# One-hots of the densest nodes and the clearing of their matrix: from VectorE to ScalarE

## The chip, the cores and the metric

The kernel runs on one core of one Trainium2 chip. The metric is the device time of one execution in microseconds (us); the figure for the kernel before is the median of 14 runs. A profile of one execution goes with it. Engines are named as in the profile: PE (TensorE, matrix products; PEld its weight loads), DVE (VectorE), ACT (ScalarE), POOL (GpSimd, which issues the indirect DMAs), SP (SyncE, which issues the plain DMAs). L971 is line 971 of the kernel before.

## What is computed

Four layers of a graph network over 12,500 nodes with 128 features and 200,000 edges; `dst` is sorted, and low-numbered nodes have many more incoming edges than high-numbered ones. Cut to what matters:

```python
edge_index = stack([src, dst])
x = layernorm(x + L0(x))     # h + out(sum over edges of filter(edge) * mlp(h)[src], at dst)
x = layernorm(x + L1(x))     # sum of x[dst] at src
x = layernorm(x + L2(x))     # sum of edge_weight * x[src] at dst, then two products, leaky relu
x = layernorm(x + L3(x))     # sum of alpha[rel] * (x @ w_rel[rel])[src] at dst, relu
```

The reference counts its layers from zero, and so do the kernel's `layers_0_and_1` and `layers_2_and_3` and this text. "Layer one" in the sense of whoever counts from one is layer zero here.

## The kernel before

**Groups and steps.** Edges go in 391 groups (`NG`) of 512 (four columns of 128, `J = 4`), from the last group to the first. `layers_0_and_1` is one long unrolled loop over steps `s`; in step `s` each stage works on another group, so that engines overlap. The order of instructions on each engine is the order in which the program issues them. An engine carries out its instructions in that order and waits at one whose inputs or buffers are not ready.

**Layer zero,** steps 0 to about 403. For the group that entered `k` steps ago: stage 2, PE computes `ph` (L783, one PSUM buffer); stage 3, ACT applies Silu (L766), and POOL gathers the source rows with four indirect DMAs (`gather`, L305) into one of seven `xg` buffers; stage 5, PE computes `pw` (L770, L773); stage 7, DVE writes the one-hots `oh` (L322) and multiplies `pw` by `xg` (L780), which frees that `xg` buffer; stage 8, PE sums by one-hots (L346); stage 11, DVE adds the result to `acc` (L371). So the gather for a group waits for the product L780 of the group seven before it. In the same loop 98 blocks of nodes are finished (`blk`, one every three steps or more), each with a Silu (L699), a square root (L639) and a scaling (L647) on ACT; Silu and square root need different tables, so each block brings two table loads. From step 21 on, 72 steps also start a DMA that fills `sums` with zeros out of a cleared part of `acc` (L403).

**Layer one,** from step 392 (`L1 = NG + 1`). For 308 groups ACT makes pairs of one-hots with `one_hots_on_act` (stage 2; L1013 to L1017: Abs, then Relu of one minus it, which is 1 where the difference is 0), PE multiplies them, ACT copies the result (`cnts`, L790, stage 5), PE multiplies again, ACT copies the messages (L833, stage 7) and POOL adds them to `sums` in DRAM with four indirect DMAs (`scatter_add`, L393, stage 8). The offsets of these, `to`, have nine buffers.

**The densest nodes.** The first 332 columns of 128 edges (`HC`) go to the nodes with the most edges. For them `DenseSteps` builds a matrix: for each column it makes two one-hots, `lo` (128 wide) for the source's place in its block and `hi` (490 wide) for the pair of source block and destination offset; PE multiplies them (L951), and DVE adds the product to a slice of `dense` (L962). `dense` is 128 partitions x 3136 f32. The columns come in 24 batches; after each, SP stores `dense` to DRAM (L967, 1568 KB) and DVE clears it (L971). This is done twice: with `kind` 0 in layer zero, where `hi` and `lo` are bf16 and the result is the plain counts for layer one; and with `kind` 1 in layer one, in f32 with the edges' weights, for layer two.

The constructor writes the order out by hand. A unit is one to four columns (or one column in two halves); one unit, or two that have four columns or fewer in all, starts every 1.68 steps for `kind` 0 and every 1.2 for `kind` 1. A unit is made in step `s`, multiplied in `s + 1`, added in `s + 2`. After the last unit of a batch, made in step `s`, the store is issued in `s + 3`, the clear in `s + 6` (`kind` 0) or `s + 5` (`kind` 1), and the next batch begins in `s + 5` or `s + 4`. `later` notes all this in two dictionaries: `taken` is run by `take` in the middle of a step, before ACT's one-hots of layer one and after its copy L790; `given` is run by `give` near the end, with `make` last. From the constants of the plan, `kind` 0 runs batches of

| batch | columns | made in steps |
|---|---|---|
| 0 | 72 | 8 to 36 |
| 1 | 28 | 41 to 51 |
| 2 | 22 | 56 to 64 |
| 3 | 18 | 69 to 75 |
| 4 | 16 | 80 to 91 |
| 5 to 23 | 176 | 96 to 365, at most 15 a batch |

For `lo` and `hi` there are four buffers each (tags `dense_lo` and `dense_hi`), one column a buffer. The lines of `make` that write them:

```python
lo = self.tile("dense_lo", P, dtype)
nc.vector.tensor_scalar(lo, c.row, ed.dense_lo[:, col:col + 1], None, op0=OP.is_equal)       # L930
hi = self.tile("dense_hi", J * P, dtype)[:, :NB * HW]
...
nc.vector.tensor_scalar(hi, self.key, ed.dense_key[:, col:col + 1], None, op0=OP.is_equal)   # L936
```

Of the kernel before, what the change touches and what calls it, by code (L numbers as in the profile page):

```python
# [8 lines left out]
F32 = mybir.dt.float32  # L9
BF16 = mybir.dt.bfloat16  # L10
I32 = mybir.dt.int32
AF = mybir.ActivationFunctionType
OP = mybir.AluOpType
# [4 lines left out]
P = 128  # L18
# [3 lines left out]
NB = 98  # L22
# [16 lines left out]
HS = 32  # L39
# [8 lines left out]
class Consts:  # L48
    def __init__(self, nc, pool):
        self.ident = pool.tile([P, P], F32, name="ident")  # L50
        make_identity(nc, self.ident)
        self.row = pool.tile([P, P], F32, name="row")
        nc.gpsimd.iota(self.row, pattern=[[1, P]], base=0, channel_multiplier=0,
                       allow_small_or_imprecise_dtypes=True)
        self.nodes = pool.tile([P, NB + 1], F32, name="nodes")
        nc.gpsimd.iota(self.nodes, pattern=[[P, NB + 1]], base=0, channel_multiplier=1,
                       allow_small_or_imprecise_dtypes=True)
        self.ones = pool.tile([P, P], F32, name="ones")
        nc.vector.memset(self.ones, 1.0)
        self.one_b = pool.tile([P, 1], BF16, name="one_b")  # L60
        nc.vector.memset(self.one_b, 1.0)
        self.eps = pool.tile([P, 1], F32, name="eps")
        nc.vector.memset(self.eps, EPS)

        self.before = pool.tile([P, P], BF16, name="before")
        nc.vector.tensor_scalar(self.before, self.row, self.nodes[:, 0:1], None, op0=OP.is_lt)
# [377 lines left out]
def kernel(ctx: ExitStack, tc: tile.TileContext, i, out):  # L444
    nc = tc.nc
    consts = ctx.enter_context(tc.tile_pool(name="consts", bufs=1))
    dram = ctx.enter_context(tc.tile_pool(name="dram", bufs=1, space=DRAM))
    c = Consts(nc, consts)
    ed = Edges(tc, c, i, consts)
# [28 lines left out]
    class Relations:  # L478
# [3 lines left out]
        def __init__(self, wk):  # L482
            self.comp = load_const(nc, wk, i["L3_gnn_compT"], [NBASIS, NREL], "comp", nc.scalar)
            self.flat = i["L3_gnn_weight"].rearrange("b d o -> b (d o)")
# [376 lines left out]
    class DenseSteps:  # L861
# [4 lines left out]
        def __init__(self, dn, ps, dense, fixed, first_weights, first_products):  # L866
            self.dn, self.ps, self.dense, self.fixed = dn, ps, dense, fixed
            self.key = dn.tile([P, NB * HW], F32, name="dense_row", tag="dense_row", bufs=1)
            nc.gpsimd.iota(self.key, pattern=[[1, NB * HW]], base=0, channel_multiplier=0,
                           allow_small_or_imprecise_dtypes=True)  # L870
            self.offs = Bases(nc.vector, ed.dense_off, "dense_off", HS - HW)
            self.degs = Bases(nc.vector, ed.dense_base, "dense_deg")
            self.rows = Bases(nc.sync, ed.dense_base, "dense_win")
            self.taken, self.given = {}, {}
            self.made, self.sums, self.ones = {}, {}, {}
            self.chunk, self.line, self.turned, self.at, self.out = {}, {}, {}, {}, {}

            for kind, t, apart, rate in ((0, 8.0, 4, 1.68), (1, first_weights, 3, 1.2)):
                for b, units in enumerate(DENSE):
                    k = 0  # L880
                    while k < len(units):
                        n = 2 if k + 1 < len(units) and units[k][1] * units[k + 1][1] and \
                            units[k][1] + units[k + 1][1] <= 4 else 1
                        s = int(t)
                        for u in units[k:k + n]:
                            self.later(self.given, s, self.make, kind, u)
                            self.later(self.given, s + 1, self.multiply, kind, u)
                            self.later(self.taken, s + 2, self.add, kind, u)
                        k += n
                        t += rate  # L890
                    self.later(self.given, s + 3, self.store, kind, b)
                    self.later(self.taken, s + apart + 2, self.clear)
                    t = s + 1 + apart
            for r in range(ROUNDS):
                start = first_products + r * (NB + 8)
                self.later(self.given, start - 3, self.load_rows, r)
                for k, h in enumerate(reversed(range(NB))):
                    if h % 2:
                        self.later(self.given, start + k, self.load, r, h - 1)
                    self.later(self.taken, start + k + 3, self.line_up, h)  # L900
                    self.later(self.given, start + k + 3, self.turn, h)
                    self.later(self.taken, start + k + 4, self.copy, h)
                    self.later(self.given, start + k + 5, self.product, h)
                    self.later(self.taken, start + k + 6, self.add_rows, h)
            self.end = max(max(self.taken), max(self.given))
# [17 lines left out]
        def make(self, kind, unit):  # L923
            c0, n = unit
            n = n or 1
            dtype = F32 if kind else BF16
            made = self.made[c0] = []
            for col in range(c0, c0 + n):
                lo = self.tile("dense_lo", P, dtype)
                nc.vector.tensor_scalar(lo, c.row, ed.dense_lo[:, col:col + 1], None, op0=OP.is_equal)  # L930
                hi = self.tile("dense_hi", J * P, dtype)[:, :NB * HW]
                if kind:
                    nc.vector.tensor_scalar(hi, self.key, ed.dense_key[:, col:col + 1], ed.dense_w[:, col:col + 1],
                                            op0=OP.is_equal, op1=OP.mult)
                else:
                    nc.vector.tensor_scalar(hi, self.key, ed.dense_key[:, col:col + 1], None, op0=OP.is_equal)  # L936
                made.append((lo, hi))
            if kind:
                ones = self.ones[c0] = self.dn.tile([P, J, HW], BF16, name="dense_one", tag="dense_one", bufs=4)
                for j in range(n):  # L940
                    nc.vector.tensor_scalar(ones[:, j, :], c.row[:, :HW], ed.dense_at[:, c0 + j:c0 + j + 1], None,
                                            op0=OP.is_equal)
# [24 lines left out]
            nc.sync.dma_start((weights if kind else counts)[b * P:(b + 1) * P, :],  # L967
                              self.dense.rearrange("p h n -> p (h n)"))

        def clear(self):  # L970
            nc.vector.memset(self.dense, 0.0)  # L971

        def load_rows(self, r):
            self.nodes = self.dn.tile([P, HK, D], F32, name="dense_x", tag="dense_x", bufs=1)
# [741 lines left out]
```

## Time and profile before

| what | value |
|---|---|
| median of 14 runs | 8075.14 us (8069.44 to 8083.61) |
| the profiled execution | 8082.02 us, its span 8080.2 us |
| busy: PE, DVE, ACT, POOL | 72%, 50%, 33%, 76% of the span |
| `lo` on DVE, L930, bf16 | 332 instructions, 293 ns each |
| `hi` on DVE, L936, bf16 | 332 instructions, 490 ns each |
| clear of `dense` on DVE, L971 | 48 instructions, 2672 ns each, 24 in each of the two layers |
| gathers of layers zero and two, L305 | 2796 instructions, 972 ns each |
| scatters of layer one, L393 | 1232 instructions, 1553 ns each |

Layer zero's gathers run from 78 to 2101 us, layer one's scatters from 2114 to 4421 us; layers two and three fill the rest. In a row of the timeline come start, duration (us), engine, line, operation, what it writes and reads, how many, and in brackets how long the engine was idle before it and what ended that. "issue" means that the profile shows nothing that the engine waited for. In a row of the waits come who waited, for whom, the sum in us, how often, and the longest.

### The profile page before, as it was taken

What the parts mean: (1) busy time and instruction counts of PE and PEld (TensorE: products, weight loads), DVE (VectorE), ACT (ScalarE), POOL (GpSimd) and SP (SyncE); (2) the same over time, 40 slices, a digit from 0 to 9 for tenths busy, and PEclk for the clock granted to TensorE, in tenths of its full rate; (3) what the DMA queues carried; (4) which work ended last, traced back from release to release, by engine and by line L of the source; (5) the groups of instructions that cost most, each with busy time, mean ns of one, the idle gap of its engine ahead of it and who ended that gap; (6) DMA issues with size and microseconds to landing.
All of it is one profiled execution on the core that took longest, in us unless ns stands there. A gap on an engine that the chain in (4) does not pass through costs nothing.

```text
span 8080.2 us, 89625 instructions
## 1 busy us (share of the span) xinstructions
PE 5827.1 (72%) x24309; PEld 3804.2 (47%) x24309; DVE 4070.6 (50%) x14132; ACT 2626.8 (33%) x5986; POOL 6117.8 (76%) x5603
## 2 busy tenths in 40 slices
PE   8889888888778766777643677777776666666665
PEld 5555555555445444554332345444443444444433
DVE  6776666554566555445431544545444443433333
ACT  2333333221578776777663311111110000000000
POOL 4777777777788888888887477777776777777777
PEclk8888878887888887777655888897875555555555
DMA  4543333333467677776665766664442222222222
GB/s 149 175 152 99 98 98 93 97 92 93 84 120 138 123 129 126 123 130 112 102 90 75 215 170 172 170 171 137 131 128 71 59 58 58 57 56 55 55 54 51
DMA packets 877254, 882.01 MB, mean 109 GB/s; under 512 B 428178, under 2 KB 683625, under 8 KB 870599
## 3 DMA queue, kind: packets, MB, share of 16 engines
q0 software_dynamic: 316960, 366.85, 25.1%
q1 hardware_dynamic: 545705, 496.90, 20.4%
q10 hardware_dynamic: 14078, 12.43, 0.5%
q8 instruction: 202, 3.31, 0.2%
q14 instruction: 309, 2.52, 0.1%
HBM read 555.71 MB, written 319.97 MB: 108 GB/s over the span
## 4 chain that ended last, share of the span: by engine, by line
POOL 27%; PE 20%; DMA 20%; issue 18%; DVE 10%; ACT 3%; DVEq 1%; SPq 0%; ACTq 0%; POOLq 0%
POOL xg L305 20%; POOL sums L393 7%; DMA xg<-table,at 6%; DMA sums<-xg,to 6%; DMA xg<-rel_table,at 6%; PE pa L346 5%; PE du L951 3%; PE pw L773 3%; PE pr L1161 2%; PE ph L783 2%; DVE dense L962 2%; DVE dense L971 1%; DVE acc L371 1%; DMA sums<-acc 1%; PE dense_sums L1212 1%
## 5 line engine op out<-in xcount | busy, mean ns | idle before, releaser
L305 POOL DMA_INDIRECT xg<-table,at x2796 | 2718.0, 972 | 953.1 <-issue 744.6
L346 PE MATMUL pa<-oh,xg 128*128 128x128 f32 x5592 | 1695.4, 420 | 1052.6 <-DMA xg<-rel_table,at 622.0
L393 POOL DMA_INDIRECT sums<-xg,to x1232 | 1913.5, 1553 | 414.1 <-issue 290.1
L346 PEld LDWEIGHTS pa<-oh,xg 128*128 128x128 f32 x5592 | 1192.2, 275 | 1636.2 <-issue 732.9
L305 POOL DMA_INDIRECT xg<-rel_table,at x1564 | 1483.4, 948 | 477.0 <-issue 370.9
L371 DVE TENSOR_TENSOR acc<-acc,pa 128x128 f32 x1090 | 305.9, 281 | 1453.6 <-PE pa L346 1403.4
L328 DVE TENSOR_SCALAR oh<-row,drel,wgt 128x128 f32<-128x128 f32 x2796 | 790.0, 357 | 36.3 <-PE pa L346 29.3
L951 PE MATMUL du<-dense_hi,dense_lo 128*128 128x490 f32 (+3 forms) x1239 | 701.8, 658 | 74.5 <-DVE dense L962 72.4
L647 ACT ACTIVATE x<-x,off,rs 128x128 f32<-128x128 f32 x294 | 144.9, 493 | 1373.0 <-DVE off L646 1363.2
L830 PE MATMUL fixed<-oh,one_b 128*1 128x128 bf16 x1216 | 145.0, 256 | 596.3 <-DVE m L1021 592.1
L783 PE MATMUL ph<-dt,fw 50*128 50x512 f32 x782 | 503.6, 728 | 79.1 <-ACT h L766 71.3
L773 PE MATMUL pw<-fw,h 128*128 128x128 f32 x3128 | 555.9, 332 | 0.0
L773 PEld LDWEIGHTS pw<-fw,h 128*128 128x128 f32 x3128 | 469.2, 230 | 118.9 <-issue 118.6
L346 PE MATMUL pa<-oh,m 128*128 128x128 f32 x3128 | 505.4, 315 | 11.0 <-DVE acc L371 10.9
L346 PEld LDWEIGHTS pa<-oh,m 128*128 128x128 f32 x3128 | 473.9, 232 | 12.4 <-DVE acc L371 11.8
L639 ACT ACTIVATE rs<-mv,eps 128x1 f32<-128x1 f32 x294 | 86.8, 295 | 1205.5 <-DVE mv L634 1187.5
L962 DVE TENSOR_TENSOR dense<-dense,du 128x490 f32 x646 | 427.8, 662 | 90.1 <-PE du L954 70.1
L1013 ACT ACTIVATE oh<-row,drel 128x128 bf16<-128x128 f32 x1216 | 388.6, 394 | 222.5 <-PE fixed L830 220.6
L1026 DVE TENSOR_TENSOR to<-n_ahead,at 128x4 int32<-128x4 f32 x308 | 50.6, 164 | 809.3 <-DMA sums<-xg,to 803.2
L780 DVE TENSOR_TENSOR m<-pw,xg 128x512 f32<-128x512 f32 x391 | 267.7, 685 | 365.2 <-DMA xg<-table,at 345.7
L766 ACT ACTIVATE h<-ph,fb 128x512 f32<-128x512 f32 x391 | 266.6, 682 | 533.5 <-PE ph L783 531.6
L1161 PE MATMUL pr<-wrel,x 128*128 128x512 f32 x784 | 429.0, 675 | 2.3 <-ACT x L1153 2.3
(205 smaller groups left out, 8449.4 us busy)
## 6 DMA issues: line engine op xcount, KB each, us to landing
rel_table<-tb SPq DMA_DIRECT2D x196, 512.0 KB
dt<-in_src_r SPq DMA_DIRECT2D x308, 256.0 KB
xg<-table,at POOLq DMA_INDIRECT x2796
dt<-in_dfT SPq DMA_DIRECT2D x391, 100.0 KB
dense_counts<-dense SPq DMA_DIRECT2D x24, 1568.0 KB
dense_in<-dense_counts SPq DMA_DIRECT2D x98, 384.0 KB
dense_weights<-dense SPq DMA_DIRECT2D x24, 1568.0 KB
dense_w_in<-dense_weights SPq DMA_DIRECT2D x96, 384.0 KB
```

Source lines behind the costliest of these rows:

```text
L305: nc.gpsimd.indirect_dma_start(out=x[:, j, :], out_offset=None, in_=table, in_offset=bass.IndirectOffsetOnAxis(ap=idx[:, j:j + 1], axis=0))
L328: nc.vector.tensor_scalar(oh[:, j, :], c.row, at[:, j:j + 1], weight[:, j:j + 1], op0=OP.is_equal, op1=OP.mult)
L346: self.nc.tensor.matmul(pa, x[:, j, :], oh[:, j, :], start=j == 0, stop=j == J - 1)
L371: nc.vector.tensor_add(to, to, pa)
L393: nc.gpsimd.indirect_dma_start(out=accs[(first + j) % len(accs)], out_offset=bass.IndirectOffsetOnAxis(ap=to[:, j:j + 1], axis=0), in_=msg ...
L773: nc.tensor.matmul(pw[:, j, :], h[:, j * P:(j + 1) * P], w.fw2, start=False, stop=j == J - 1)
L780: nc.vector.tensor_mul(ms[g], pws.pop(g), xgs.pop(g))
L783: nc.tensor.matmul(phs[g], w.fw1, dts.pop(g), start=True, stop=True)
L951: nc.tensor.matmul(pk[:, :NB * HW], lo[part], hi[part], start=j == 0, stop=j == len(made) - 1)
L962: nc.vector.tensor_tensor(to, to, pk[:, :NB * HW].rearrange("p (h n) -> p h n", n=HW), op=OP.add)
L1013: nc.scalar.activation(pair[:, 0, j, :], c.row, AF.Abs, bias=at[:, j:j + 1], scale=-1.0)
L1161: nc.tensor.matmul(pr, t["x3"], wrel[:, k:k + 4, :], start=True, stop=True)
```

## The change

In `make`, for `kind` 0 alone, DVE's two comparisons a column become four activations on ACT: for `lo` and for `hi`, the absolute difference, and then in place Relu of one minus that. For `kind` 1 the two comparisons stay on DVE. In both kinds the clear of `dense` becomes two copies on ACT of a constant zero column, one for each half of the matrix (1568 elements a partition each); the first half is cleared one step earlier than the whole was, the second half in the step in which the whole was.

```diff
+        self.zero = pool.tile([P, 1], F32, name="zero_c")
+        nc.vector.memset(self.zero, 0.0)
...
-                    self.later(self.taken, s + apart + 2, self.clear)
+                    self.later(self.taken, s + apart + 1, self.clear, 0)
+                    self.later(self.taken, s + apart + 2, self.clear, 1)
...
                 lo = self.tile("dense_lo", P, dtype)
-                nc.vector.tensor_scalar(lo, c.row, ed.dense_lo[:, col:col + 1], None, op0=OP.is_equal)
                 hi = self.tile("dense_hi", J * P, dtype)[:, :NB * HW]
                 if kind:
+                    nc.vector.tensor_scalar(lo, c.row, ed.dense_lo[:, col:col + 1], None, op0=OP.is_equal)
                     nc.vector.tensor_scalar(hi, self.key, ed.dense_key[:, col:col + 1], ed.dense_w[:, col:col + 1],
                                             op0=OP.is_equal, op1=OP.mult)
                 else:
-                    nc.vector.tensor_scalar(hi, self.key, ed.dense_key[:, col:col + 1], None, op0=OP.is_equal)
+                    for to, of, at in ((lo, c.row, ed.dense_lo), (hi, self.key, ed.dense_key)):
+                        nc.scalar.activation(to, of, AF.Abs, bias=at[:, col:col + 1], scale=-1.0)
+                        nc.scalar.activation(to, to, AF.Relu, bias=c.ones[:, 0:1], scale=-1.0)
...
-        def clear(self):
-            nc.vector.memset(self.dense, 0.0)
+        def clear(self, k):
+            half = self.dense.rearrange("p h n -> p (h n)")[:, k * NB * HS // 2:(k + 1) * NB * HS // 2]
+            nc.scalar.copy(half, c.zero.to_broadcast([P, NB * HS // 2]))
```

## The prediction

> **What bounds the kernel now.** I read the page first, then the waits of GpSimd, then its instructions one by one. The page's busy shares and the first line of its chain:
>
> ```profile
> PE 5827.1 (72%) x24309; PEld 3804.2 (47%) x24309; DVE 4070.6 (50%) x14132; ACT 2626.8 (33%) x5986; POOL 6117.8 (76%) x5603
> POOL 27%; PE 20%; DMA 20%; issue 18%; DVE 10%; ACT 3%; DVEq 1%; SPq 0%; ACTq 0%; POOLq 0%
> ```
>
> POOL is 76% busy and the chain gives it 27% plus 18% of "issue". The waits of POOL and of DVE in layer zero (95 to 2070 us) say what "issue" is:
>
> ```profile
> POOL xg L305 <- issue: 404.7, 1328, 0.3
> DVE m L780 <- DMA xg<-table,at: 326.4, 165, 7.7
> ```
>
> POOL sits 0.3 us before each gather and never longer: a fixed price, not a wait. A gather is 0.944 + 0.305 = 1.25 us, four make a group, so POOL cannot do a step under 5.0 us; 391 steps are 1955 of the 1975 us. POOL bounds layer zero, and the product L780 waits for what it fetches. ScalarE is far from the bound, ACT 45 us busy in 119 to 260 us. So work that leaves DVE pays only if it reaches POOL. One thing does:
>
> ```profile
> L305 POOL DMA_INDIRECT xg<-table,at x1527: 940/944/4134, 94.3 to 2069.5; - x191
> L393 POOL DMA_INDIRECT sums<-xg,to x1209: 1541/1542/1862, 2128.9 to 4398.9; - x173
> ```
>
> and two rows of the timeline (start, duration, engine, line):
>
> ```profile
> 1190.77 4.10 POOL L305 DMA_INDIRECT xg<-table,at  x1 [0.30 <-issue]
> ...
> 1191.31 2.67 DVE L971 MEMSET dense<- 128x3136 f32 x1 [0.60 <-issue]
> ```
>
> The first fence has min/median/max of the gathers (layer zero) and of the scatters (layer one). A gather has a median of 0.944 us and a maximum of 4.13. In the timeline 22 gathers are over 2.2 us; each overlaps one of the 24 memsets of `dense`, and 22 of 22 end 0.9 us after it: 1190.77 + 4.10 = 1194.87 against 1191.31 + 2.67 = 1193.98. Together they are 58.6 us over the median. The memsets at 266.8 and 419.8 stretched nothing, nor did any of the 24 in layer one, where no scatter is over 1.86 us.
>
> **Part 1, the clears.** DVE loses 48 memsets of 2.67 us. In layer zero that gives POOL 58.6 us back if the copy on ScalarE does not hold it. Nearest row: gathers that ran beside ScalarE's Abs and Relu at 2078 to 2100 us took 0.94 us. So I book -59, with 0 as the other end.
> Here the Trainium skill speaks against the row. "SBUF — State Buffer", section "Who interferes with whom", has VectorE and GpSimd share one port pair as an exclusive lock, but says that on this chip an instruction with one SBUF input or none, outside the two-port modes, does not contend, and names a memset as contending on trn3 alone. By that rule there is no relief, and the sum below would be 8195. The trace shows 22 of 24, so I follow it. The same section has ScalarE wait for nobody.
>
> **Part 2, the one-hots.** Of 332 columns DVE loses 0.29 + 0.49 us each (L930, L936), 260 us, from an engine that waits 326 us for gathers: worth nothing. ScalarE gets four activations a column. Their price, from rows of the same Abs and Relu at the start of layer one:
>
> ```profile
> 2077.86 0.69 ACT L766 ACTIVATE h<-ph,fb 128x512 f32<-128x512 f32 x1 [2.56 <-PE ph L783]
> 2078.45 1.26 ACT L1013 ACTIVATE dense_hi<-row,drel 128x128 bf16<-128x128 f32 x4
> 2079.62 1.26 ACT L1015 ACTIVATE dense_hi<-dt,src_f 128x128 bf16<-128x128 int32 x4
> 2080.91 1.15 ACT L1017 ACTIVATE dense_hi<-dense_hi,ones 128x1024 bf16<-128x1024 bf16 x1
> 2081.97 0.28 ACT L806 ACTIVATE past<-at,nodes 128x4 f32<-128x4 int32 x1
> ```
>
> Abs follows Silu without a table load. Four narrow ones take 1.26 us, one alone 0.39 (group row L1013), so the next independent one starts after (1.26 - 0.39) / 3 = 0.29. The Relu that reads them starts 0.03 after their end. Per element, (1.148 - 0.388) / 896 = 0.85 ns, so 490 wide is 0.388 + 362 x 0.00085 = 0.69, and 0.60 to the next independent one. A column: 0.42 + 0.29 + 0.72 + 0.60 = 2.03 us. Bounds: 1.78 if nothing waits for an Abs to end, 2.16 if nothing overlaps.
> "ScalarE: Activation LUTs", section "What ACT_TABLE_LOAD costs", states 280 ns + 0.833 ns per element with a pointer bias and 93 ns of overlap back to back. That makes an estimate of 1.78 us a column, a loss of 63 us below in place of 100 and a time of 8099; the row at 2080.91 shows that Relu waits, so 2.03 stands.
>
> Where does it lie? The columns are bunched: 72 in steps 8 to 36, then 28 (41 to 51), 22 (56 to 64), 18 (69 to 75), 16 (80 to 91), and under 1.3 a step later. The stretch of the first batch, by windows (PE, PEld, DVE, ACT, POOL; clock, DMA):
>
> ```profile
> 101.00:236.00 135.00, 127.93 (x663) 82.06 (x662) 102.34 (x355) 37.30 (x54) 102.39 (x108) 0.93 0.46 135
> ```
>
> ScalarE there has 37 us. Batch 0 becomes 72 x 2.03 = 146, + 37, + 13 of waits = 196 us, where POOL needs 29 x 5.0 = 145: 51 over. The waits: only four columns' buffers exist, so of 18 units the six made one step after the last wait for PE to do ph (1.12) and its first product (0.42), some 1.7 us each with the handover, and 3 us elsewhere. Likewise, with the same windows' ACT time and 3 us for the clear before: batch 1 57 + 21 + 3 + 5 = 86 against 55, batch 2 45 + 16 + 3 + 4 = 68 against 45, batch 3 37 + 11 + 3 + 3 = 54 against 35, batch 4 32 + 25 + 3 + 2 = 62 against 60. Over: 51 + 31 + 23 + 19 + 2 = 126 us.
>
> What is queued behind: the Silu of the next group stands behind these activations on ScalarE, the next ph and pw behind it on PE, the product L780 behind those on DVE, and only that frees a buffer for POOL. POOL's cover is seven buffers: the product of group 8 (in order of processing) ends at 139.2 and the gather that reuses its buffer starts at 153.6, so the lead is 14 us at the start (28 at most later, and 5.6 for group 68, at 451). Between batches are four steps in which PE can run at 4.0 us (Silu 119.51 to 167.88 in 12 steps) against POOL's 5.0, so some 12 us are made up in three gaps. Loss for POOL: 126 - 14 - 12 = 100 us. At the lower price without the waits, the overruns are 20 + 19 + 13 + 11 and the loss 37; at 2.16 with nothing made up between batches it is 126 + 156 x 0.13 - 14 = 132. After step 92 ScalarE needs some 80% of a step, the lead grows again, and nothing more is lost; what was lost is not got back, since POOL has no idle time left in layer zero.
>
> **Part 3, the clears in layer one.** POOL is the bound again (scatter 1.54 + 0.31, four in 7.4 us). ScalarE is 312 of 400 us busy at 2300 to 2700 and now stops for the store of `dense`: its first half comes a step earlier than the memset did, right after the copy L790. In three batches the memset itself waited, so landing is known: 2303.27 to 2310.82, 2515.41 to 2523.52, 2594.87 to 2603.09, about 8 us after issue. L790 ends 0.5 to 6.6 us after the issue, so ScalarE waits 7, 2, 2, 8 and 7 us in the first five batches, 26, plus 15 of copying (1568 elements at 0.85 ns + 0.2 = 1.5 us a half). Queued behind it are the one-hots, and the message copy L833 that POOL waits for. At that time messages are 3 to 9 us ahead of POOL; later 25 to 35, enough for any such stop. Of 41 us I book half, 20; bounds 0 and 41. No scatter was held by a memset, so no relief here. Layers two and three are untouched. The added constant is one small memset before the bound starts: nothing.
>
> **Sum.** -59 + 100 + 20 = +61 us. The profiled execution took 8082.0 us (span 8080.2), 6.9 over the median of 14 runs, 8075.1; span 8141, runs 8136 us.
>
> **Rivals.**
> Faster: the overrun is absorbed. If ScalarE's batches fit (seven buffers, DVE out of PE's way, Relu not waiting), only the relief is left: 8075 - 59 = 8016. For it: the 22 stretched gathers are certain, and DVE held PE up (L951 waits 72.4 us for L962). Against: 72 columns at the lower price are 128 + 37 = 165 us in 145. It decides where a column costs under (145 + 14 - 37) / 72 = 1.69 us; the sign turns already where loss and stops together stay under 59.
> Even: a loss near 50 and no stop in layer one cancel the relief, 8065 to 8085.
> Slower still: the copy on ScalarE, or the one-hots left around it, hold gathers as the memset did: no relief, 8136 + 59 = 8195. Against: gathers at 2078 to 2100.
> That the edit does not do what it says would show as L930 and L936 still on DVE in layer zero; the diff leaves them no path there.
>
> **How the numbers follow.** My forecast (relief, and ScalarE over its steps) 0.69, 8136, own range 8050 to 8190. Faster rival 0.14; even 0.08; slower still 0.09. Its low end is 37 - 59 + 0 = -22, 8053; its high end 132 - 59 + 41 = +114, 8189. The range goes to 8045 and 8205 to take in the slower rival. What a measurement here can tell from no change is about 0.2%, 16 us (the runs spread over 14). Faster 0.18 (its rival and the low edge of mine), same 0.10, slower 0.72.
>
> **What the profile of the changed kernel would show.** Right: no gather over 1.4 us beside a clear; POOL waits of microseconds before L305, released by L780, between 150 and 600 us, some 100 us in all and none after; ACT at nine tenths in the slices to 500 us; Silu L766 there 7 us apart; layer zero ending some 40 us later; in layer one ScalarE waiting for `dense_weights` and new gaps of POOL before 2700. Wrong: POOL without such gaps (then the first rival), or gathers still stretched to 3 or 4 us at the clears (then the last), or ScalarE loading tables between Silu and Abs, which no row here shows.

## The result, and the profile after

The changed kernel takes 8159.12 us (median of 6 runs, 8150.81 to 8168.44) against 8077.2 us for the kernel before beside it: the ratio is 1.0101, 95% interval 1.0091 to 1.0111. It is slower by 82 us; the forecast was 61, and the range held it. The profiled executions differ by a little less: spans of 8153.8 and 8080.2 us, 73.6 us apart. Lines have moved: L305 is now L307, L780 is L782, L766 is L768, L783 is L785, L393 is L395, L833 is L835; the activations are L941 (Abs) and L942 (Relu), the clear is L979.

The page of the changed kernel, its busy shares, two rows of its slices (203.8 us each) and the first line of its chain:

```profile
PE 5878.6 (72%) x24309; PEld 3831.5 (47%) x24309; DVE 3751.2 (46%) x13421; ACT 3417.3 (42%) x7410; POOL 6049.1 (74%) x5603
...
ACT  5878775544467887777664311111110000000000
POOL 4457777777788888888888377777776777777777
...
POOL 25%; PE 20%; DMA 19%; issue 17%; ACT 11%; DVE 7%; DVEq 1%; SPq 0%; ACTq 0%; POOLq 0%
```

DVE lost 319 us of comparisons and memsets, ACT gained 790 us and stands at seven and eight tenths from the second to the sixth slice, and POOL, which bounds the kernel, is at four and five tenths in the second and third slice, where it had seven. The chain goes through ACT for 11% where it had 3%.

The gathers of layer zero and the scatters of layer one (min/median/max in ns, first and last start in us):

```profile
L307 POOL DMA_INDIRECT xg<-table,at x1549: 938/944/1042, 94.7 to 2175.9; - x194
```
```profile
L395 POOL DMA_INDIRECT sums<-xg,to x1232: 1541/1542/1981, 2190.3 to 4502.5; - x176
```

No gather in this view is over 1.04 us any more: the relief came, and a little more of it than forecast. The waits of POOL from 95 to 2200 us say what it was spent on:

```profile
POOL xg L307 <- issue: 413.9, 1358, 0.3
POOL xg L307 <- DVE m L782: 138.4, 43, 8.1
POOL xg L307 <- DVE acc L373: 25.9, 21, 8.2
```

The fixed 0.3 us before each gather is there as before; new are 138.4 us of waits for the product L782 and some that are put down to `acc`. Gap by gap, what exceeds 0.31 us before a gather sums to 0.0 us before and 144.7 us after, in 34 gaps. Counted along POOL, layer zero is 66.5 us better (stretched gathers 58.6 to 0, small excesses over 0.944 us 11.3 to 3.4) and 144.7 worse. Compared group by group, the changed kernel is behind by 9 us after 24 groups of four gathers, 48 after 40, 109 after 64, 133 after 88, and then gains back to 76 at the last, as the stretches that it no longer has fall due. In layer one the distance stays 76 us from the first scatter to the last (before, these started at 2113.7 and 4426.6 us).

The first batch in windows (columns as shown before), and ACT's own waits over batches 0 to 4:

```profile
99.80:313.90 214.10, 161.12 (x662) 97.99 (x662) 64.99 (x228) 179.92 (x343) 123.77 (x131) 0.76 0.32 94
```

```profile
ACT h L768 <- PE ph L785: 40.8, 23, 3.9
ACT hb L701 <- DVE x L708: 35.4, 12, 8.9
ACT dense_lo L941 <- PE du L957: 25.4, 12, 3.5
ACT x L649 <- DVE off L648: 12.1, 5, 3.3
```

ACT is busy 179.9 of 214.1 us in the stretch that had been 145 us, and in the 580 us of the five batches it waits 114 us, 66 of them for PE. How this reaches POOL is seen in the longest waits of PE and of DVE, from 100 to 660 us:

```profile
PE ph L785 <- ACT h L768: 127.9, 36, 8.7
DVE acc L373 <- PE pa L348: 245.4, 41, 10.3
```

Before, from 95 to 590 us, the two were 34.7 and 59.2 us. PE waits for ACT's Silu; the sums `pa` stand behind `ph` in PE's order; DVE stands at the add of `pa` to `acc`, and behind that add stands L782, which frees the gather's buffer. L782 does not wait for its own input: before each of the 34 gaps its `pw` had been done for 8 to 20 us.

How ACT and PE hold each other up is seen in the timeline where one unit of four columns ends (first ACT's rows alone, then some rows of each engine):

```profile
206.06 0.39 ACT L941 ACTIVATE dense_lo<-row,dense_lo 128x128 bf16<-128x128 f32 x1
206.48 0.40 ACT L942 ACTIVATE dense_lo<-dense_lo,ones 128x128 bf16<-128x128 bf16 x1
206.78 0.69 ACT L941 ACTIVATE dense_hi<-dense_row,dense_key 128x490 bf16<-128x490 f32 x1
207.51 0.70 ACT L942 ACTIVATE dense_hi<-dense_hi,ones 128x490 bf16<-128x490 bf16 x1
208.12 0.39 ACT L941 ACTIVATE dense_lo<-row,dense_lo 128x128 bf16<-128x128 f32 x1
...
213.19 0.69 ACT L768 ACTIVATE h<-ph,fb 128x512 f32<-128x512 f32 x1
213.92 0.94 POOL L307 DMA_INDIRECT xg<-table,at  x1 [1.01 <-DVE m L782]
213.93 2.07 PE L785 MATMUL ph<-dt,fw 50*128 50x512 f32 x2 [5.38 <-ACT h L768]
215.93 1.41 PE L957 MATMUL du<-dense_hi,dense_lo 128*128 128x490 bf16 x3
...
216.56 0.40 ACT L941 ACTIVATE dense_lo<-row,dense_lo 128x128 bf16<-128x128 f32 x1 [2.68 <-PE du L957]
```

A column takes 2.06 us, from 206.06 to 208.12. The whole unit, with the two table loads behind it, delays the Silu of the next group to 213.19; PE had waited 5.38 us for it, and then the one PSUM buffer of `ph` lets PE do one product and no more. ACT in its turn waits 2.68 us for the products L957 that free a `dense_lo` buffer. Neither can work ahead of the other.

In the runs e5 to e8 and e12 the kernel before took 9176 us in place of 8074 to 8078, as DVE waited for something outside the profile ("remote", 689 us before L371 in e6) and POOL had some 600 us of gaps in layer zero; from these I read only single gathers and scatters, and layer one, where POOL's gaps are 23 to 30 us as in the other runs.

### The profile page after: what moved, and what is told of

Its sections match the earlier page's. It is cut to its first block, busy times and chain, and to the rows that moved or that the text cites. A ratio compares the mean times of both kernels' runs of the same rounds, so it can differ in the third digit from the quotient of the medians.

```text
span 8153.8 us, 90401 instructions
## 1 busy us (share of the span) xinstructions
PE 5878.6 (72%) x24309; PEld 3831.5 (47%) x24309; DVE 3751.2 (46%) x13421; ACT 3417.3 (42%) x7410; POOL 6049.1 (74%) x5603
## 4 chain that ended last, share of the span: by engine, by line
POOL 25%; PE 20%; DMA 19%; issue 17%; ACT 11%; DVE 7%; DVEq 1%; SPq 0%; ACTq 0%; POOLq 0%
POOL xg L307 18%; POOL sums L395 7%; DMA sums<-xg,to 6%; DMA xg<-table,at 5%; DMA xg<-rel_table,at 5%; PE pa L348 5%; PE du L957 3%; PE ph L785 3%; PE pw L775 3%; PE pr L1169 2%; ACT dense_hi L942 2%; ACT dense_hi L941 1%; DVE dense L968 1%; ACT dense_lo L942 1%; ACT h L768 1%
## 5 line engine op out<-in xcount | busy, mean ns | idle before, releaser
L307 POOL DMA_INDIRECT xg<-table,at x2796 | 2650.4, 948 | 1097.7 <-issue 750.7
L395 POOL DMA_INDIRECT sums<-xg,to x1232 | 1912.3, 1552 | 415.0 <-issue 286.5
L307 POOL DMA_INDIRECT xg<-rel_table,at x1564 | 1483.6, 949 | 477.1 <-issue 375.5
L957 PE MATMUL du<-dense_hi,dense_lo 128*128 128x490 f32 (+3 forms) x1239 | 710.6, 669 | 28.1 <-DVE dense L968 28.0
L785 PE MATMUL ph<-dt,fw 50*128 50x512 f32 x782 | 516.2, 744 | 200.3 <-ACT h L768 192.6
L768 ACT ACTIVATE h<-ph,fb 128x512 f32<-128x512 f32 x391 | 266.6, 682 | 391.5 <-PE ph L785 390.2
L782 DVE TENSOR_TENSOR m<-pw,xg 128x512 f32<-128x512 f32 x391 | 267.3, 684 | 317.4 <-DMA xg<-table,at 288.5
```

Of the source, the lines that this page charges most:

```text
L307: nc.gpsimd.indirect_dma_start(out=x[:, j, :], out_offset=None, in_=table, in_offset=bass.IndirectOffsetOnAxis(ap=idx[:, j:j + 1], axis=0))
L395: nc.gpsimd.indirect_dma_start(out=accs[(first + j) % len(accs)], out_offset=bass.IndirectOffsetOnAxis(ap=to[:, j:j + 1], axis=0), in_=msg ...
L768: nc.scalar.activation(hs[g], phs.pop(g), AF.Silu, bias=w.fb1)
L785: nc.tensor.matmul(phs[g], w.fw1, dts.pop(g), start=True, stop=True)
L957: nc.tensor.matmul(pk[:, :NB * HW], lo[part], hi[part], start=j == 0, stop=j == len(made) - 1)
```

## The experiments

No run leaves out any of the work. Each ratio is to the kernel before as it ran beside: 8074.15 us for e1 to e4, 8077.52 for e9 to e11, 9176 for the others.

The theory after the result: ACT's units of four columns hold up layer zero's first 92 steps, and the clears on ACT give the relief. Rivals: the latency that four activations in place of two comparisons add to each column; a cost of each moved column wherever it lies; and, for the relief, that something other than the memset held the gathers.

### Each part alone (e1, e2)

e1, the clears alone; e2, the one-hots alone, with the memset back on DVE:

```diff
# e1, against the change
-                    for to, of, at in ((lo, c.row, ed.dense_lo), (hi, self.key, ed.dense_key)):
-                        nc.scalar.activation(...)   # Abs, Relu
+                    nc.vector.tensor_scalar(lo, c.row, ed.dense_lo[:, col:col + 1], None, op0=OP.is_equal)
+                    nc.vector.tensor_scalar(hi, self.key, ed.dense_key[:, col:col + 1], None, op0=OP.is_equal)
# e2, against the change
-            nc.scalar.copy(half, c.zero.to_broadcast([P, NB * HS // 2]))   # two halves
+            nc.vector.memset(self.dense, 0.0)                              # one clear
```

> The clears on ScalarE as in the change, the one-hots of the counts back on VectorE. My theory: the memset on VectorE is what held the gathers, so no gather is over 1.4 us, POOL never waits for L780, and the time is that of before less 59 to 67 us: 8010 to 8018. Rival 1, the relief in the changed kernel came from the one-hots that left VectorE, not from the clears: gathers are stretched as before or half as much, 8045 to 8077. Rival 2, ScalarE's stop for the store of the matrix costs layer one what the prediction booked: 20 us more, 8030 to 8038.

> The one-hots on ScalarE as in the change, the clears back on VectorE in one memset, at their old step. My theory: the loss of 145 us by ScalarE's overrun in steps 8 to 92 stays whole, and the gathers beside the memsets after step 92 are stretched as before (some 50 us; the earlier ones fall where POOL is held anyway): 8200 to 8225. Rival, ScalarE's clears and their wait are a good part of the overrun: the gaps of POOL before L305 fall to 120 us or less and the time to 8170 to 8195.

e1 took 8026.11 us, ratio 0.9937 (0.992 to 0.9954): 48 us faster than the kernel before, and 8 us short of what I expected. In its trace no gather of layer zero takes over 1.23 us, POOL has no gap there, and the layer ends 57 us earlier. e2 took 8171.44 us, ratio 1.0118 (1.0102 to 1.0135). Its gaps sum to 138 us of the change's 145, so the loss is the one-hots'. But I had expected 50 us of stretch with the memsets back, and there were 21.8, in 9 gathers of 24 memsets. The maximum shows that the stretch is there:

```profile
L307 POOL DMA_INDIRECT xg<-table,at x1548: 938/944/4055, 95.3 to 2191.2; - x194
```

In the timeline of e2 one memset that stretched nothing, and one that did (rows of DVE and POOL):

```profile
540.64 2.67 DVE L976 MEMSET dense<- 128x3136 f32 x1 [0.60 <-issue]
541.12 0.94 POOL L307 DMA_INDIRECT xg<-table,at  x1 [0.30 <-issue]
542.37 0.94 POOL L307 DMA_INDIRECT xg<-table,at  x1 [0.30 <-issue]
543.23 0.23 DVE L708 SCALAR_TENSOR_TENSOR x<-x,fixed 128x128 f32<-128x128 f32 x1
...
766.73 2.67 DVE L976 MEMSET dense<- 128x3136 f32 x1 [0.60 <-issue]
767.25 3.04 POOL L307 DMA_INDIRECT xg<-table,at  x1 [0.30 <-issue]
769.32 0.75 DVE L324 TENSOR_SCALAR oh<-row,drel 128x128 f32<-128x128 f32 x4
```

The memsets are the same, 0.60 us after the add to `acc`. What differs is the next instruction of DVE: 0 of 15 memsets followed by a reciprocal or a scalar_tensor_tensor held a gather, 9 of 9 followed by a tensor_scalar did. Before, all 24 memsets of layer zero had a tensor_scalar behind them (L930, once L322) and all 24 of layer one a tensor_tensor. That made a new question, taken up below.

### Where the loss comes from (e3, e4, e7, e11)

e3: `lo` on ACT, `hi` on DVE. e4: the change, with a unit of batches 0 to 3 every 2.5 steps. e7 and e11, the same kernel: the columns below 156 on DVE.

```diff
# e3
+                    nc.scalar.activation(lo, ...)   # Abs, Relu
+                    nc.vector.tensor_scalar(hi, self.key, ed.dense_key[:, col:col + 1], None, op0=OP.is_equal)
# e4
-                        t += rate
+                        t += rate if kind or b > 3 else 2.5
# e7, e11
-                if kind:
+                if kind or col < 156:
```

> As the change, but only the narrow one-hot (128 wide) is made on ScalarE; the wide one (490) stays on VectorE. A column costs ScalarE some 0.72 us in place of 2.06, so the first batch needs 72 x 0.72 = 52 + 37 = 89 us in 145. My theory, the loss is work over the step: nothing is lost and the time is that of the clears alone, 8010 to 8020. Rival, the loss is latency, since what PE waits for now stands behind Silu in ScalarE's order: a third or more of the 145 us stays, 8060 or more.

> As the change, but the first four batches of the counts start a unit (or pair) every 2.5 steps in place of 1.68, which moves the later batches back by some 29 steps. The first batch then has 45 steps, 225 us, for 146 of one-hots, some 58 of the rest and some 20 of waits. My theory, the loss is ScalarE's work over the steps given to it: it falls from 145 to under 25 us, 8010 to 8040. Rival, the loss comes with each column, by the order of waits between ScalarE and PE, however far apart the columns lie: the gaps of POOL stay over 70 us, 8085 or more.

> The change, with the columns below 156 (batches 0 to 4, the bunched ones of steps 8 to 91) made on VectorE as before; the 176 later columns and all clears stay on ScalarE. Theory (the loss comes only from steps in which four columns hold ScalarE for 8.2 us at over 1.3 columns a step): no gap of POOL over 5 us in all in layer zero, the relief stays whole, 8020 to 8032 us. Rival (each column moved costs something wherever it lies): 176 of 332 columns keep half of the loss, 60 to 80 us, 8085 to 8110 us.

> The change with the columns below 156 made on VectorE, once more, for its time on another chip: no gap of POOL over 5 us in all in layer zero, ratio 0.993 to 0.9955. Rival (each column moved costs something wherever it lies, 176 of 332): ratio 1.001 to 1.005.

e3 took 8027.94 us (ratio 0.9938, 0.9922 to 0.9955), with no gap of POOL: half of the work on ACT costs nothing, though what PE needs for a column still stands behind the Silu in ACT's order, so a latency from that order alone falls. e7, beside 9176 us, gave 0.999 (0.9968 to 1.0012) and decides nothing. e11 took 8018.69 us (0.9928, 0.9911 to 0.9944). POOL's waits in its layer zero, 95 to 2030 us, hold nothing over 0.3 us:

```profile
POOL xg L307 <- issue: 404.1, 1326, 0.3
POOL xg L307 <- DMA xg<-table,at: 15.5, 51, 0.3
POOL xg L307 <- DVE oh L324: 15.5, 51, 0.3
POOL xg L307 <- DVE acc L373: 5.5, 18, 0.3
```

So 176 of 332 columns, with all four activations each, are free on ACT, and the other 156, the bunched ones, carry the whole loss. The free ones come one or two to a step: such steps take 5.5 and 6.6 us in e11, and the lead on POOL, over 12 us there, takes that up.

e4 took 8101.8 us (ratio 1.0034, 1.0021 to 1.0046), against the 8010 to 8040 that I expected; it is what the rival on record for it had, 8085 or more with gaps over 70 us. Spread to 2.5 steps, the four columns and the rest of ACT's work are 4 x 2.06 + 2.5 x 1.3 = 11.5 us in 12.5, and yet POOL lost 87 us in gaps:

```profile
POOL xg L307 <- issue: 393.8, 1292, 0.3
POOL xg L307 <- DVE m L782: 82.2, 34, 8.0
POOL xg L307 <- DVE acc L373: 22.9, 24, 6.9
```

The table tells why. It counts the steps from 8 to 109 (Silu to Silu) by the columns made in them:

| kernel | steps with 4 columns | mean us | steps with none | mean us | ACT busy in these |
|---|---|---|---|---|---|
| before | (DVE) | | 102 | 4.99 | 1.69 |
| change | 34 | 10.8 | 50 | 3.45 | 1.64 |
| e4 | 34 | 9.9 | 64 | 3.76 | 1.8 |
| e3 (`lo` alone) | 34 | 6.7 | 50 | 3.63 | 1.64 |

A unit falls into one step. That step takes some ten microseconds, and a step without columns is not over when ACT's 1.64 us are done, but after 3.45 in the mean (1.9 to 9.8); PE is busy for 2.9 of these. How much of them is PE's own work, held up before, and how much the passing of the group to and fro was not measured apart. PE's work also grew: in the windows of the first batch 662 products took 161.1 us of it, and 663 took 127.9 before, at a granted clock of 0.76 against 0.93. So the time of a stretch is not ACT's work in it summed, but that of its steps one by one. For the change, 34 x 10.8 + 50 x 3.45 + 123 for the 18 steps with one to three columns = 663 us, where POOL needs 102 x 5.0 = 510; less the lead of 14, a loss of 139, measured 144.7. For e4, 34 x 9.9 + 64 x 3.76 + 30 for four more = 607, less 510 and 14: 83, measured 87.3. For e3 the same sum is 34 x 6.7 + 50 x 3.63 + 95 = 504, under 510: no loss. These are sums of measured steps: they show that POOL's gaps are what the long steps cost over its pace less what the short ones give back, and forecast nothing. A unit spread evenly over its steps, the direct test, was not tried. Not tried either was the DMA that fills `sums` with zeros out of `acc`: DVE's add to `acc` waited 57.6 us for it from 100 to 660 us, against 40.6 in all of layer zero before; in e3 it waited 40.9 us and POOL lost nothing.

### What held the gathers (e5, e10, e6, e9, e12, e8)

Each is the kernel before, with one instruction behind the memset, or another one in its place:

```diff
             nc.vector.memset(self.dense, 0.0)
+            nc.vector.reciprocal(self.plug, c.ones[:, 0:1])                        # e5, e10: 128x1, all 48
+            nc.vector.tensor_scalar(self.lure, c.row[:, :64], ..., op0=OP.is_equal)  # 128x64; e6: layer one, e9: layer zero
+            nc.vector.tensor_scalar(c.before, c.row, ..., op0=OP.is_lt)             # e12: 128x128, all 48
# e8
-            nc.vector.memset(self.dense, 0.0)
+            nc.vector.tensor_tensor(self.dense, self.dense, self.dense, op=OP.subtract)
```

> The kernel before, with one thing added: behind each memset of dense VectorE gets a reciprocal of 128x1 into a tile that nothing reads. All 48 memsets and all one-hots stay on VectorE. Theory (a gather is held not by the memset but by a tensor_scalar that stands next in VectorE's queue behind it: before, 22 of 24 memsets with a tensor_scalar next stretched a gather, and of those followed by a reciprocal, a scalar_tensor_tensor or a tensor_tensor none did): at most 2 gathers stretched, 50 to 60 us less than before, 8015 to 8026 us, as when the clears went to ScalarE. Rival (the memset itself holds the gather): 20 or more gathers stretched, 8070 to 8082 us. Third (the hold moves to the tensor_scalar that stands one place later, still dispatched during the memset): 20 or more stretched as well, by some 2.7 us each.

> The kernel with a reciprocal of 128x1 behind each memset once more, for its time on another chip: no stretched gather, and where POOL has no gaps in layer zero 50 to 60 us less than before (ratio 0.9925 to 0.994), with ScalarE given no work. Rival (the memset costs something besides the stretch, or a tensor_scalar two places behind holds as well): ratio over 0.997.

In e5 and e10 no memset holds a gather, though all of them are still on DVE; the longest gather of e10's layer zero is 1.2 us:

```profile
L305 POOL DMA_INDIRECT xg<-table,at x1549: 943/947/1205, 94.1 to 2043.5; - x194
```

e10 took 8023.09 us, ratio 0.9933 (0.9917 to 0.995): the whole gain of e1, for 48 instructions of 0.1 us and no work for ACT. e5, beside 9176 us, gave 0.9988 (0.9971 to 1.0006), and its time decides nothing. So the memset by itself holds nothing.

> The kernel before, with one thing added in layer one alone: behind each of the 24 memsets of dense there VectorE gets a tensor_scalar of 128x64 (is_equal, into a tile that nothing reads). There the instruction behind the memset was a tensor_tensor so far and no scatter was stretched. Theory (the waiting tensor_scalar holds GpSimd): 18 to 24 scatters stretched by 2 to 3 us, 45 to 65 us more in layer one, of which POOL's 25 us of gaps there take up a part: 8100 to 8135 us. Rival (memsets hold gathers from the table and not scatters, whatever comes next): no scatter over 1.9 us, 8070 to 8082 us.

> The kernel before, with the tensor_scalar of 128x64 that did nothing behind the memsets of layer one now put behind the 24 memsets of layer zero instead. Theory (any waiting tensor_scalar holds a gather from the table, and the scatters of layer one are another matter): of the memsets that overlap a gather nearly all stretch it by 2 to 3 us, 20 or more of 24 where POOL is not waiting, time within 10 us of before. Rival (that small tensor_scalar does not hold GpSimd at all, the one-hot's does for its size or for its buffers): 0 to 3 stretched, 50 to 60 us less than before.

My theory missed both. In e6 no scatter was held (time ratio 1.0007, 0.9988 to 1.0026), while in its layer zero, left as before, 16 of the 16 memsets that ran beside a gather held it:

```profile
L393 POOL DMA_INDIRECT sums<-xg,to x1232: 1542/1543/1918, 2714.2 to 5027.2; - x176
```

```profile
2988.05 2.67 DVE L972 MEMSET dense<- 128x3136 f32 x1 [1.06 <-DMA dense_weights<-dense]
...
2988.44 1.54 POOL L393 DMA_INDIRECT sums<-xg,to  x1 [0.31 <-ACT oh L1020]
...
2990.29 1.54 POOL L393 DMA_INDIRECT sums<-xg,to  x1 [0.30 <-issue]
2990.64 0.13 DVE L974 TENSOR_SCALAR lure<-row,dense_lo 128x64 bf16<-128x64 f32 x1
```

The tensor_scalar `lure` stands right behind the memset, and two scatters pass at 1.54 us. In e9, with that instruction in layer zero, the gathers were free too, and the time was 8020.51 us, ratio 0.9933 (0.9916 to 0.9949):

```profile
L305 POOL DMA_INDIRECT xg<-table,at x1550: 940/944/1245, 94.4 to 2042.3; - x194
```

So it was not the scatters that made the difference, but the instruction: this one of 128x64 holds nothing, nor does the one-hot of 128x128 that now stands one place further back. The last run put one of 128x128 there, which waits for no other engine and which no one waits for.

> The kernel before, with a tensor_scalar of 128x128 (bf16 from f32, the size of the one-hot dense_lo) behind all 48 memsets: it writes the constant before once more with the values it has. In layer zero it stands ahead of the one-hot, as the one of 128x64 did that took the stretch away. Theory (a waiting tensor_scalar holds GpSimd if it is as wide as a one-hot; 64 wide it does not): in layer zero 20 or more of 24 stretched as before, and in layer one 18 to 24 scatters stretched by 2 to 3 us, 45 to 65 us more there: 8100 to 8140 us. Second theory (width decides, and scatters are not held whatever waits): 20 or more gathers, no scatter, 8070 to 8082 us. Rival (it is not the width; only an instruction of the one-hots' own holds): no gather stretched, 8015 to 8030 us.

```profile
L305 POOL DMA_INDIRECT xg<-table,at x1548: 938/945/4001, 94.8 to 2665.8; - x194
```
```profile
L393 POOL DMA_INDIRECT sums<-xg,to x1232: 1542/1543/4511, 2696.5 to 5061.5; - x176
```

```profile
2966.66 2.67 DVE L971 MEMSET dense<- 128x3136 f32 x1 [0.60 <-issue]
...
2967.69 3.14 POOL L393 DMA_INDIRECT sums<-xg,to  x1 [0.30 <-issue]
...
2969.26 0.16 DVE L972 TENSOR_SCALAR before<-row,nodes 128x128 bf16<-128x128 f32 x1
...
2971.13 1.54 POOL L393 DMA_INDIRECT sums<-xg,to  x1 [0.30 <-issue]
```

That is the first theory, in both layers: 15 of the 15 memsets beside a gather hold it, and 24 of 24 in layer one hold a scatter, for 53 us in all; layer one is 52 us longer than in e6. The time ratio is 1.0067 (1.0044 to 1.0091). In the rows the scatter starts at 2967.69, 1.03 us after the memset, and ends at 2970.83, 1.57 after the tensor_scalar begins, as if it had begun there.

> The kernel before, with dense cleared on VectorE by a tensor_tensor (dense minus dense, two inputs in SBUF) in place of the memset; the next instruction is a tensor_scalar as before. Theory (what holds the gather is the tensor_scalar that waits, whatever it waits behind): about 22 gathers in layer zero stretched for as long as this instruction lasts, 3 to 4 us, so 60 to 85 us of stretch against 58.6, none in layer one, 8075 to 8105 us. Rival (it is the memset's own zeros, written without an input, that hold it): no gather stretched, 8015 to 8030 us.

e8 agrees in layer zero (16 of 16 held, 40 us) and misses in layer one, where it held 24 of 24, 51.4 us, with a tensor_tensor next:

```profile
L971 DVE TENSOR_TENSOR dense<-dense x48: 3407/3418/3480, 359.6 to 4776.7; 128x3136 f32<-128x3136 f32 x48
```

```profile
L393 POOL DMA_INDIRECT sums<-xg,to x1232: 1541/1542/4501, 2726.2 to 5092.2; - x176
```

A clear that reads two inputs from SBUF holds a scatter by itself; a memset of 2.67 us does not. Its ratio was 1.0049 (1.003 to 1.0068).

Over all runs, memsets of `dense` beside a gather or scatter: with a 128x128 tensor_scalar next on DVE 86 of 88 held it by over 0.5 us (22 of 24 before, 9 of 9 in e2, 16 of 16 in e6, 39 of 39 in e12), with anything else next 0 of 222. The two that held nothing, at 267 and 420 us before, have a wait on one and the same semaphore at that tensor_scalar; the only other with it, at 351, held for half as long (1.35 us). That this wait is the reason was not tried. The tensor_scalar of 128x64 that held nothing is an is_equal from f32 to bf16 like the one-hot L930, half as wide and with an output that nothing reads; why that is too little, and where the border lies, stays open too.

## Why the prediction was right, and where it was not

**POOL bounds, and ACT's overrun reaches it: right.** All 34 gaps lie between 165 and 666 us, each ends as a product L782 does, and none follows. e2 has the loss without the clears on ACT, e11 has these and no loss. One link was otherwise than I wrote: I had L780 wait for `pw`, and it waits behind DVE's add to `acc`, which waits for `pa`.

**The price of a column: right.** Booked 2.03 us, measured 2.06; the Relu starts 0.03 to 0.04 us after its Abs ends, at 206.48 after 206.45. The 1.78 us of the other estimate is not seen.

**The loss, 100 booked, 145 measured: the term of the waits.** I added to each batch's activations a few waits (13, 5, 4, 3 and 2 us) and compared the sum with POOL's 5.0 us a step. The overruns were to be 51, 31, 23, 19, 2; measured by the Silus they are 69, 35, 30, 22, 7, and 5 in batch 5, 168 in place of 126. A sum lets ACT use the short steps in full to catch up what a long step lost, and the table of steps shows that it can't: they take 3.45 us in the mean where ACT has 1.64 us of work. The steps between batches, for which I booked 12 us, gave 6 up to batch 4 and 6 more behind it. So 168 - 14 - 12 = 142. ACT stands at seven and eight tenths where I had nine; the rest is its waits. The bound of 132 was too low for the same reason; e4, which the same sum called free, lost 87.

**The relief, 59 booked, 66 measured: right size, wrong cause.** I read 22 of 24 as the memset's own doing, against the rule of the Trainium skill ("SBUF — State Buffer", section "Who interferes with whom") that a memset does not contend here while a tensor_scalar can. As to the memset the runs agree with the rule, with 0 of 222. The relief came true only because the change took the memset, or the tensor_scalar behind it, away. The row that I passed over was in my own text: "nor any of the 24 in layer one" asks what is different there. The 50 us that I expected of e2 fell by the same step.

**Layer one, 20 booked, 0 measured.** The stop is there, larger than forecast:

```profile
ACT dense L979 <- DMA dense_weights<-dense: 54.3, 21, 6.8
```

54.3 us of waits for the store before the first halves, besides 48 copies of 1.5 us. But who needs ACT there, POOL for its messages (L835), did not wait longer than before (the first row is the kernel before):

```profile
POOL sums L393 <- ACT xg L833: 7.8, 18, 1.8
POOL sums L395 <- ACT xg L835: 6.5, 19, 1.0
```

POOL's gaps in layer one sum to 25.9 us, and to 25.3 before. Once started, the messages' lead on POOL never ran out: at its lowest it was 2.8 us, at the 32nd and 56th group. Half of a bound was booked with no row for it; the lead of 3 to 9 us that the prediction names was enough each time.

**The sum.** -66.5 + 144.7 + 0 = 78; layer zero starts 2 us earlier and layers two and three give 2, so the span is 74 longer. The loss was booked 45 too small, the relief 7 too small and layer one 20 too large: 61 + 45 - 7 - 20 = 79, so the errors in part cancelled. **The rivals:** "absorbed" (8016) is what e1, e3 and e11 are, each with a load on ACT that fits the step; "slower still" fell with the gathers at 0.944 us beside the clears.

## What to carry to other kernels

Between engines that hand one buffer to and fro, add up a stretch step by step, the longest engine of each step, and not one engine's work over the stretch: work that comes in lumps costs its excess over the pace, beyond what the lead of the buffers takes up, even where the mean fits. Before you move an instruction that seems to hold another engine, look at the one that stands behind it in the queue, and find the cases in which nothing was held: here one reciprocal of 0.1 us behind each memset (e10, 8023 us) was worth as much as moving the clears (e1, 8026) or moving clears and late columns (e11, 8019), and all three beat the kernel before, by 48 to 59 us, and the change by over 130.

## What the hardware showed that was not expected

A tensor_scalar of 128x128 that stands behind a memset on DVE holds POOL's indirect DMAs while it waits, by 0.7 to 3.2 us each and 2.4 in the mean of 86, and one of 128x64 does not (0 of 48). A tensor_tensor of 128x3136 with two inputs in SBUF (3.42 us) holds scatters itself, 24 of 24, by 0.9 to 3.0 us. A clear on ACT held none: in the change the longest gather beside one took 0.95 us, the longest scatter 1.82.

After an idle time of 5.4 us the product `ph`, 1.12 us in PE's busy stretches, took 2.07, and 2.04 to 2.07 after each of the eight idle times of over 5 us in the change; in the first batch PE was granted 0.76 of its clock, against 0.93 before. That this lengthens ACT's waits for PE is likely; its share of the loss was not measured by itself.
